# Layer 0's recurrent loop: the order of two transposes, two products on another engine, and the step that makes the gate's products

## The chip, the cores and the metric

The kernel runs on one core of a Trainium2 chip. A core has four compute engines that matter here, each with its own in-order instruction stream: TensorE (PE; its weight loads appear as PEld), VectorE (DVE), ScalarE (ACT) and GpSimd (POOL). SyncE (SP) issues most DMAs. The metric is the device time of one execution in microseconds; lower is better. The kernel before takes 4783.76 us, the median of three runs (4769.75 to 4790.43).

## The reference

Four layers, each with an attention-like part `s` and a feed-forward part whose silu is its gate; the residual `x` becomes `x + s * silu(f)`. Only layer 0 is touched by the change. Its attention part is a state-space recurrence over 512 tokens, with a batch of 8; its feed-forward part is a mixture of eight experts that does not depend on the recurrence at all:

```python
def step(carry, inp):
    state, y_prev = carry
    xBC = silu(xBC_t + y_prev @ W_rxbc.T)
    dtr = silu(dt_t + y_prev @ W_rdt.T)
    ...
    dt = softplus(dtr + dt_bias); dA = exp(dt * A)
    state = state * dA + dt * x_h * B
    y = (state * C).sum(-1) + D_param * x_h
    g = y * silu(z_t)
    yn = g * rsqrt(mean(g * g) + EPS) * norm_w
    return (state, yn), yn @ W_out.T
...
h = relu(einsum('etd,efd->etf', xn, w1) + b1)
y = x + einsum('etf,edf->etd', h, w2) + b2
```

Each step needs the `yn` of the step before it, so the 512 steps are one serial chain.

## The kernel before

`layer0` walks `step(t)` for t = 0 to 511 under a manual schedule: within the loop each engine's instructions stand in the order in which the code writes them. The expert network's work is spread through the loop to fill TensorE's spare time, and whatever of it is left when the last step is issued is made by `ffn.rest` behind the loop. Then the loop's outputs are projected (L546), scaled (L549) and gated into the residual (`gate_residual`, L51 to L53); layer 1 starts from that residual.

**One step.** The last result, `yh` (L414), feeds `norm` and the recurrent product on TensorE (L221). GpSimd makes the root `rh` (L283), VectorE adds up the row `a` (L317), ScalarE applies silu (`ar`, L323), VectorE turns it (`h`, L325). From `h` come `cb` (L339) and `Z`; TensorE sums `cb` into `pag` (L354) and multiplies `Z` with the saved state into `pym` (L361, 64 records). GpSimd meanwhile makes `v`, `e`, `e` and `dec` (L332 to L350), the decay; then `xd` (L351), `zd` (L352) and, late, the new column of `xw` (L402). VectorE ends the step with a run of small operations: `tmp`, its sums `R`, `M`, the turned step size `td`, the turned decay `dA`, the turned state product `ty` (which reads `pym`), then products and sums into the next `yh`, and last the decay of the history `xw` (L423).

The state is not updated in each step. The kernel keeps a history of up to `past` tokens and folds it into the saved state once in eight steps. `past` runs from 5 to 12. A step is **long** where `past` > 8: these are the steps with t % 8 of 1, 2, 3 and 4 from t = 9 on, 252 of them. In long steps the sums `R` are taken in two halves, with `td` between them, and the folding is made: GpSimd's `decayed` (L490) runs at "half 0" ahead of `v`, TensorE's products `us` (L479) at "update".

**The fillers on TensorE.** At "products" each step asks `ffn.products` for up to four matmuls (not where t % 8 is 0) and fills up to seven with `occupy`, matmuls whose result nobody reads. Behind the state product it calls `aside(t)`, in steps that have no `us` products or whose t % 16 is in `ASIDE`, and fills up to four with `occupy`. `aside` makes one of three things: a group of the next projections (`ASIDE` 0 to 3), the two products of the gate z two chunks ahead (`ASIDE` 4; their silu is queued in `gates` for the next two steps), or another call of `ffn.products`.

**The expert network.** 256 jobs (eight experts, 32 token tiles), each of four hidden products with four RELUs on ScalarE (L673, L683), four output products (L656) and one add on VectorE (L691). One call of `products` gives at most four matmuls: either hidden columns or one job's outputs. `activate(RELUS[t % 8])` is at most 18 RELUs in eight steps.

Of the kernel before, what the change touches and what calls it, by code (L numbers as in the profile page):

```python
# [11 lines left out]
ALU = mybir.AluOpType  # L12
# [45 lines left out]
PC = 8  # L58
TC = 16
Q = 8  # L60
ASIDE = {5: 0, 7: 1, 13: 2, 15: 3, 9: 4}
CAP = 40.0
RELUS = [2, 1, 1, 1, 2, 4, 4, 3]
LAG = 5
# [74 lines left out]
def layer0(tc, K, I, dr, xn, s_all, s_out, x, B, T):  # L139
# [10 lines left out]
    nc = tc.nc  # L150
    ident, eps = K["ident"], K["eps"]
    with ExitStack() as ctx:
# [42 lines left out]
        xw = wp.tile([P, 2, B, 32], F32, name="xw")  # L195
        SINCE = (0, 2 * Q + 1)
# [8 lines left out]
        pa, pg, py, pm = pag[:, 0:RW], pag[:, 256:384], pym[:, 0:64], pym[:, 64 : 64 + B]  # L205
# [6 lines left out]
        tt_, stt_ = nc.vector.tensor_tensor, nc.vector.scalar_tensor_tensor  # L212
# [10 lines left out]
        def occupy(n, where):  # L223

            for _ in range(n):
                nc.tensor.matmul(where, ident, K["ones"], start=True, stop=True)  # L226
# [4 lines left out]
        def aside(t):  # L231

            c, r = t // TC + 2, t % TC
            if c * TC < T and r in ASIDE:
                j = ASIDE[r]
                if j == 4:
                    for k in range(2):
                        proj.gate(c, k, ring[k])
                        gates.append(lambda k=k: proj.silu(c, k, ring[k]))
                    return 2  # L240
                proj.group(c, j, ring[j % 2])
                if j == 3:
                    proj.dt(c, pdt)

                def kept():
                    proj.keep(c, j, ring[j % 2])
                    if j == 3:
                        proj.send(c, pdt)

                sums.append((t, kept))  # L250
                return 4
            return ffn.products(t, sums)
# [5 lines left out]
        def turned(src, n, name):  # L258
            t = wk.tile([P, n, 32], F32, name=name)
            nc.vector.transpose(out=t, in_=src)  # L260
            return t

        def small(name, n=2, bufs=2):
            return wk.tile([P, n, B], F32, name=name, bufs=bufs)

        def one_(name):
            return wk.tile([P, 1], F32, name=name)

        def both(v):

            return v.unsqueeze(1).to_broadcast([P, 2, B])
# [15 lines left out]
        def part(t, place):  # L287
            f = parts.pop((t, place), None)
            if f:
                f()  # L290
            return f is not None

        def held(t):

            return max(0, (t - LAG) // Q)
# [6 lines left out]
        def step(t, rt, zt):  # L302
# [23 lines left out]
            now = slice(B * s, B * s + B)  # L326
            C, x = h[:, 0, now], h[:, 2:4, now]
            part(t, "half 0")
            v, dt, dec = one_("v"), one_("dt"), one_("dec")
            e, w, ad = one_("e"), one_("w"), one_("ad")  # L330

# [12 lines left out]
                o += hi - lo  # L344
            nc.vector.tensor_copy(bass.AP(z9.tensor, z9.offset, [list(z9.ap[0]), [9, B]]), C)
            tt_(w, v, Acap, ALU.mult)
            xz, xd, zd = small("xz"), small("xd"), small("zd")
            tt_(xz, x, zt, ALU.mult)
            tt_(ad, w, A, ALU.min)
            nc.gpsimd.tensor_tensor(dec, e, ad, ALU.pow)  # L350
            nc.gpsimd.tensor_tensor(xd, xz, Dp, ALU.mult)  # L351
            nc.gpsimd.tensor_tensor(zd, xw[:, :, :, SINCE[held(t) % 2]], zt, ALU.mult)  # L352
            for j in range(4):
                nc.tensor.matmul(  # L354
                    pg[32 * j : 32 * j + 32, 0 : B * o], K["ones"][:, 0:32], cb[:, 0 : B * o], start=True, stop=True
# [9 lines left out]
            given = 4 if part(t, "update") else 0  # L365
            if not given or t % TC in ASIDE:
                given += aside(t)
# [11 lines left out]
            M = small("M")  # L379

            def total(c):
                nc.vector.tensor_reduce(out=R[:, c], in_=tmp[:, c, :, 0:past], op=ALU.add, axis=AX.X)  # L382

            spread = lambda v, name: turned(v.to_broadcast([P, 32]), 1, name)[:, 0, 0:B]
            long = past > Q
# [5 lines left out]
            td = both(spread(dt, "td"))  # L391
            if long:
                total(1)
            dA = both(spread(dec, "dA"))
            tt_(M, M, td, ALU.mult)
            if long:
                tt_(R, R, zt, ALU.mult)
            occupy(4 - given, pag[:, 384:])
            part(t, "copies")
            ffn.activate(RELUS[t % Q])  # L400
# [1 line left out]
            nc.gpsimd.tensor_tensor(xw[:, :, :, s + 1], td, x, ALU.mult)  # L402
            part(t, "half 1")

            ty = turned(py.rearrange("p (c e) -> p c e", e=32), 2, "ty")
            y = small("y")
            if past:
                tt_(R, R, dA, ALU.mult)
            tt_(zd, zd, dA, ALU.mult)
            tt_(M, M, xd, ALU.add)  # L410
            tt_(y, zd, ty[:, :, 0:B], ALU.mult)
            if past:
                tt_(M, M, R, ALU.add)
# [110 lines left out]
        with tc.manual_schedule():  # L524
            for t in range(T):
                if t % PC == 0:
                    cur = nxt
                    if t + PC < T:
                        nxt = piece(t // PC + 1)
                if t % Q == Q - 1 and t + 1 + LAG < T:  # L530
                    update(t // Q)
                part(t, "start")
                step(t, cur[:, t % PC, :], proj.z[t // TC][:, :, t % TC, :])
            norm(T - 1)
            ffn.rest(sums)
# [1043 lines left out]
```

## Time and profile before

| what | value |
|---|---|
| median of three runs | 4783.76 us |
| the profiled execution | 4780.57 us |
| its span | 4778.8 us |
| PE busy | 4390.6 us (92%) |
| DVE busy | 3478.5 us (73%) |
| ACT busy | 3292.8 us (69%) |
| POOL busy | 2374.4 us (50%) |
| first and last start of `yh` | 123.1 and 2814.4 us |

The profile has one row for each kind of instruction or for each stretch of a timeline: start or count, duration, engine, line of the kernel, operation, output and inputs. A bracket says how long the engine had been idle and what released it. On TensorE one fp32 matmul of the code leaves two records, so the 1024 hidden products appear as 2048. The loop, from the first `yh` to the last, takes 2691.3 us, 5.27 us a step.

### The profile page before, as it was taken

Reading aid. Unit: us, or ns where it says so; the run is one execution under the profiler, and the core shown is the slowest. Engines: PE = TensorE matmul, PEld = TensorE weight load, DVE = VectorE, ACT = ScalarE, POOL = GpSimd, SP = SyncE. Lnnn points to the kernel's source line nnn. Section 1 sums busy time; section 2 is a strip of 40 time slices with the busy share of each in tenths; the row PEclk is TensorE's granted clock in tenths of the full one; section 3 lists DMA queues with packets and bytes.
Section 4 is the critical chain, followed back from the end, with each engine's and each line's share of the span. In section 5 each row is a group of like instructions: output and inputs, shape, how many; then the busy total and the mean of one; then the engine's idle time right before and its main releaser. Section 6 shows DMA issues by size and latency. Waiting matters only on the chain.

```text
span 4778.8 us, 193203 instructions
## 1 busy us (share of the span) xinstructions
PE 4390.6 (92%) x79351; PEld 3273.0 (68%) x79351; DVE 3478.5 (73%) x18350; ACT 3292.8 (69%) x6513; POOL 2374.4 (50%) x5479
## 2 busy tenths in 40 slices
PE   6999999999999999999999987969999888999998
PEld 5777777777777777777777764325556555666666
DVE  4788888888888888888888876457776336777781
ACT  2788888888888888888888854436666124666665
POOL 1555555555555555555555544420001355778782
PEclk6999999999999999999999998869999998999999
DMA  3000000000000000000000032000000520000000
GB/s 93 12 9 16 9 11 14 8 11 13 11 9 16 8 9 16 9 10 15 9 10 9 9 60 66 18 1 2 2 2 2 107 56 1 2 2 2 2 2 18
DMA packets 72713, 81.39 MB, mean 17 GB/s; under 512 B 8844, under 2 KB 55057, under 8 KB 71699
## 3 DMA queue, kind: packets, MB, share of 16 engines
q1 hardware_dynamic: 67116, 65.04, 5.6%
q8 instruction: 622, 10.19, 0.9%
q10 hardware_dynamic: 4710, 3.99, 0.3%
q14 instruction: 265, 2.16, 0.2%
HBM read 52.72 MB, written 16.29 MB: 14 GB/s over the span
## 4 chain that ended last, share of the span: by engine, by line
PE 44%; DVE 34%; POOL 10%; ACT 6%; issue 5%; DMA 1%; SPq 0%; ACTq 0%; POOLq 0%; DVEq 0%
PE pt L959 7%; POOL rh L283 5%; PE ps_s L938 4%; PE pag L354 4%; PE pym L221 4%; DVE a L317 3%; PE po L973 3%; DVE h L325 3%; ACT ar L323 3%; DVE tmp L374 3%; DVE R L382 3%; DVE cb L339 3%; DVE yh L414 2%; PE ph L673 2%; PE py L1126 2%
## 5 line engine op out<-in xcount | busy, mean ns | idle before, releaser
L216 ACT ACT_TABLE_LOAD x1024 | 1313.8, 1283 | 16.5
L283 POOL TENSOR_TENSOR rh<-ms,half 128x1 f32<-128x1 f32 x512 | 280.3, 548 | 708.5 <-DVE ms L280 707.9
L361 PE MATMUL pym<-S,Z 128*8 128x64 f32 x32768 | 551.9, 219 | 0.1
L1257 POOL TENSOR_SCALAR gp<-toe,ng 128x207 f32<-128x207 f32 (+1 forms) x512 | 489.7, 965 | 111.2 <-DVE mn L946 73.3
L959 PE MATMUL pt<-ident,sb 128*128 128x128 f32 x3328 | 498.4, 283 | 13.0 <-ACT pT L962 8.1
L959 PEld LDWEIGHTS pt<-ident,sb 128*128 128x128 f32 x3328 | 356.5, 141 | 208.2 <-ACT pT L964 78.5
L361 PEld LDWEIGHTS pym<-S,Z 128*8 128x8 f32 x32768 | 489.2, 90 | 0.1
L323 ACT ACTIVATE ar<-a 128x129 f32<-128x129 f32 x511 | 159.6, 312 | 437.3 <-DVE a L317 437.1
L962 ACT COPY pT<-pt 128x512 f32<-128x512 f32 (+3 forms) x512 | 255.5, 499 | 243.5 <-PE pt L959 242.2
L226 PE MATMUL pym<-ones,ident 128*128 128x128 f32 x2942 | 417.4, 277 | 0.0
L946 DVE CUSTOM_DVE_ANT_0 sb<-ps_s,gp 128x512 f32<-128x512 f32 x512 | 324.1, 685 | 101.1 <-PE ps_s L938 86.2
L226 PEld LDWEIGHTS pym<-ones,ident 128*128 128x128 f32 x2942 | 369.7, 192 | 0.4 <-DVE ms L280 0.4
L221 PE MATMUL pag<-w_Wr,yh 128*8 128x129 f32 x8176 | 352.0, 277 | 0.0
L952 ACT ACTIVATE sb<-sb,mn 128x512 f32<-128x512 f32 (+3 forms) x512 | 330.6, 646 | 22.9 <-DVE mn L946 17.3
L221 PEld LDWEIGHTS pym<-yh 128*8 128x8 f32 x8192 | 172.6, 154 | 223.8 <-DVE yh L414 215.7
L317 DVE SCALAR_TENSOR_TENSOR a<-pag,rh,rows 128x129 f32<-128x129 f32 x511 | 180.6, 353 | 197.7 <-POOL rh L283 194.6
L683 ACT ACTIVATE hid<-ph,be 128x128 f32<-128x128 f32 x1024 | 311.2, 360 | 12.1 <-PE ph L673 11.9
L221 PE MATMUL pym<-yh 128*8 128x8 f32 x8192 | 231.5, 220 | 85.8 <-DVE yh L414 61.7
L350 POOL TENSOR_TENSOR dec<-e,ad 128x1 f32<-128x1 f32 x512 | 286.5, 560 | 43.6 <-POOL e L334 1.1
L673 PE MATMUL ph<-xhT,ew 128*128 128x128 f32 x2048 | 308.1, 291 | 0.0
L333 POOL TENSOR_TENSOR e<-base,v 128x1 f32<-128x1 f32 x512 | 280.9, 549 | 40.1
L497 ACT ACTIVATE Sd<-S,das 128x64 f32<-128x64 f32 x1008 | 298.2, 397 | 3.0
(365 smaller groups left out, 10551.1 us busy)
## 6 DMA issues: line engine op xcount, KB each, us to landing
cB<-dc SPq DMA_DIRECT2D x16, 1024.0 KB
pd<-stg SPq DMA_DIRECT2D x32, 258.0 KB
rows<-pd SPq DMA_DIRECT2D x256, 32.2 KB
wu<-in_f_up_dram SPq DMA_DIRECT2D x9, 512.0 KB
wd<-in_f_down_dram SPq DMA_DIRECT2D x9, 512.0 KB
rd<-rv SPq DMA_DIRECT2D x1, 3304.0 KB
x<-in_u_dram SPq DMA_DIRECT2D x8, 256.0 KB
w<-in_f_w_dram SPq DMA_DIRECT2D x8, 256.0 KB
```

Of the source, the lines that this page charges most:

```text
L216: nc.scalar.preload_act_table_set(name)
L221: nc.tensor.matmul(out[32 * j : 32 * j + B, :], lhsT, rhs(j), start=(k == 0), stop=(k == 1))
L226: nc.tensor.matmul(where, ident, K["ones"], start=True, stop=True)
L283: nc.gpsimd.tensor_tensor(rh[:, t : t + 1], ms, half, ALU.pow)
L317: stt_(a, pa, rh[:, t - 1 : t], rt, ALU.mult, ALU.add)
L361: nc.tensor.matmul(py[32 * j : 32 * j + B, :], z9[:, B * b : B * b + B], Sq[b % 4][:, b // 4, :, 32 * j : 32 * j + 32], start=(i == 0), st ...
L673: self.nc.tensor.matmul(self.ph[:, f, :], self.w[n][0][:, f * P : (f + 1) * P], self.xhT[:, i * P : (i + 1) * P], start=True, stop=True)
L683: self.nc.scalar.activation(self.hid[n][:, f, :], self.ph[:, f, :], AF.Relu, bias=self.be[:, self.jobs[n][0], f : f + 1])
L946: nc.vector.tensor_tensor_reduce(out=sb[:, 0:L], in0=ps[:, g, 0:L], in1=bias[g], scale=1.0, scalar=3.0e38, op0=ALU.add, op1=ALU.min, accum ...
L952: nc.scalar.activation(sb[:, 0:L], sb[:, 0:L], AF.Exp, scale=-1.0, bias=mn)
L959: nc.tensor.transpose(pt[:, j * P : (j + 1) * P], sb[:, j * P : (j + 1) * P], self.ident)
L1257: nc.gpsimd.tensor_scalar(t[:, k0:k1], toe[:, h, o : o + k1 - k0], gates[b][:, i, h : h + 1], None, ALU.mult)
```

## The change

Five edits in `layer0`:

- The gate's two products move from the steps with t % 16 = 9 to those with t % 16 = 0.
- `zd` on GpSimd is made behind "half 0", ahead of `v`, instead of behind `xd`.
- In steps that are not long, `ty` is turned ahead of `dA`.
- In long steps `M * td` and `M + xd` are made on GpSimd, directly after one another, instead of on VectorE.
- In long steps `ty` keeps its place; in the others both products of M stay on VectorE.

```diff
-ASIDE = {5: 0, 7: 1, 13: 2, 15: 3, 9: 4}
+ASIDE = {0: 4, 5: 0, 7: 1, 13: 2, 15: 3}
...
             part(t, "half 0")
+            zd = small("zd")
+            nc.gpsimd.tensor_tensor(zd, xw[:, :, :, SINCE[held(t) % 2]], zt, ALU.mult)
...
-            xz, xd, zd = small("xz"), small("xd"), small("zd")
+            xz, xd = small("xz"), small("xd")
...
             nc.gpsimd.tensor_tensor(xd, xz, Dp, ALU.mult)
-            nc.gpsimd.tensor_tensor(zd, xw[:, :, :, SINCE[held(t) % 2]], zt, ALU.mult)
...
             if long:
                 total(1)
+            turned_y = lambda: turned(py.rearrange("p (c e) -> p c e", e=32), 2, "ty")
+            if not long:
+                ty = turned_y()
             dA = both(spread(dec, "dA"))
-            tt_(M, M, td, ALU.mult)
             if long:
+                nc.gpsimd.tensor_tensor(M, M, td, ALU.mult)
+                nc.gpsimd.tensor_tensor(M, M, xd, ALU.add)
                 tt_(R, R, zt, ALU.mult)
+            else:
+                tt_(M, M, td, ALU.mult)
...
-            ty = turned(py.rearrange("p (c e) -> p c e", e=32), 2, "ty")
+            if long:
+                ty = turned_y()
...
-            tt_(M, M, xd, ALU.add)
+            if not long:
+                tt_(M, M, xd, ALU.add)
```

## The prediction

> **What bounds the kernel now.** The first view is the slice row of the page: layer 0's loop fills slices 2 to 24 of 40. The timeline's `yh` rows give 2691.3 us from first to last, 5.27 us a step. PE looks 90% busy there, but much of that is `occupy`, which fills waiting time, so busy shares say little. I therefore read the chain of waits over a stretch with a gate step (t % 16 = 9):
>
> ```profile
> 1515.21 0.89 PE pym L361 x64
> 1516.11 1.06 PE us L479 x4
> 1517.16 0.64 PE paside L131 x4
> 1517.80 0.42 PE pym L221 x10
> ```
>
> Columns: start, length, what. Here TensorE decides: the gate's products (L131) stand between the folding products and the next step's L221. Everywhere else the step is a chain through all engines whose end is VectorE's run of small operations. A long step on VectorE, and below it GpSimd beside it (start, length, engine, line, operation, output and inputs):
>
> ```profile
> 1521.48 0.20 DVE L260 STREAM_TRANSPOSE td<-dt 128x32 f32<-128x32 f32 x1
> 1521.61 0.20 DVE L382 TENSOR_REDUCE R<-tmp 128x8 f32<-128x80 f32 x1
> 1521.72 0.20 DVE L260 STREAM_TRANSPOSE dA<-dec 128x32 f32<-128x32 f32 x1
> 1521.85 0.18 DVE L395 TENSOR_TENSOR M<-M,td 128x16 f32<-128x16 f32 x1
> 1521.95 0.16 DVE L397 TENSOR_TENSOR R<-R,z 128x16 f32<-128x16 f32 x1
> 1522.04 0.24 DVE L260 STREAM_TRANSPOSE ty<-pym 128x64 f32<-128x64 f32 x1
> 1522.20 0.13 DVE L408 TENSOR_TENSOR R<-R,dA 128x16 f32<-128x16 f32 x1
> 1522.26 0.16 DVE L409 TENSOR_TENSOR zd<-zd,dA 128x16 f32<-128x16 f32 x1
> 1522.34 0.17 DVE L410 TENSOR_TENSOR M<-M,xd 128x16 f32<-128x16 f32 x1
> 1522.45 0.17 DVE L411 TENSOR_TENSOR y<-zd,ty 128x16 f32<-128x16 f32 x1
> 1522.54 0.17 DVE L413 TENSOR_TENSOR M<-M,R 128x16 f32<-128x16 f32 x1
> 1522.75 0.19 DVE L414 TENSOR_TENSOR yh<-y,M 128x16 f32<-128x16 f32 x1
> ```
>
> ```profile
> 1521.07 0.56 POOL L350 TENSOR_TENSOR dec<-e,ad 128x1 f32<-128x1 f32 x1
> 1521.60 0.22 POOL L351 TENSOR_TENSOR xd<-xz,w_Dp 128x16 f32<-128x16 f32 x1
> 1521.78 0.23 POOL L352 TENSOR_TENSOR zd<-xw,z 128x16 f32<-128x16 f32 x1
> 1521.96 0.24 POOL L402 TENSOR_TENSOR xw<-td,h 128x16 f32<-128x16 f32 x1
> ```
>
> The starts matter, not the lengths. Independent operations start 0.05 to 0.17 us apart; a dependent one starts 0.03 after the other's end: `zd` to `y` is 0.19, `M+R` to `yh` 0.21. What follows the loop is the third view:
>
> ```profile
> 2816.09 10.86 PE L546 MATMUL po<-w_WoT,yh 128*128 128x128 f32 x94
> 2837.16 1.26 POOL L53 TENSOR_TENSOR x<-x,gate 128x512 f32<-128x512 f32 x1
> ```
>
> The last `yh` starts at 2814.36. TensorE projects, and GpSimd's eight gate chunks end at 2838.42, 24.06 us later. No expert work is left by then: the last output product starts at 2805.7.
>
> **Edit 1, the gate's step.** From `yh` to L221 it takes 0.24 us normally and 0.65 after t % 16 = 9 (median of 31), and the rest of the next step (1.32 to `rh`, 0.73 to `ar`) is alike, so all 0.41 comes back. In t % 16 = 9 of the last two chunks an expert call stands in the gate's place, which goes too: 32 x 0.41 = **13 us** gained. In t % 16 = 0 two gate products and two `occupy` replace four matmuls: nothing. The silus of the gate now stand in the ACT streams of t % 16 = 1 and 2, ahead of `ar`; ACT is idle 0.56 to 1.2 us before `ar` in such steps and a silu takes 0.28: nothing.
>
> **But the call is lost to the experts.** At t % 16 = 9 the gate sat in a step that already had `us`; at 0 it takes the place of `ffn.products`. Calls in 16 steps: 14 at "products", four in `aside` (t % 16 = 0, 6, 8, 14), together 18; eight jobs need 16 full ones. After it 17 are left, and some are short because hidden columns may run only four ahead of the RELUs. I stepped the counters (`cols`, `relus`, `outs`) of both through the loop: before, 256 jobs are out at the last step; after, seven instead of eight in 16 steps, and at the end 918 columns and 228 jobs. The changed kernel's instruction order says the same: behind the last step stand 107 hidden and 112 output products, mixed with 57 projections. Inside the loop `occupy` takes their places, so nothing is saved there.
>
> Price: 276 matmuls are 552 records. L546 ran 94 in a row, loads 10.67 us, 0.1135 each: 62.7 us. They start 0.6 after the last `yh` and end at +63.5 (two jobs of lead, so no RELU holds them: four take 1.12 us beside 2.27 us of PE per job with its projections). Then the last add 0.35, its gate silu 0.63, two GpSimd operations of 1.27 and gaps: +67.3, against 24.1. That is **+43 us**. ACT's 12 weight DMA issues (6.6 us in all) formerly lay in gaps; in the new order they stand behind the last gate silu, ahead of a 1.28 us table load and layer 1's root. About 4 us were free there; I take +3 (0 to 4). Tail **+46** (42 to 50).
>
> **Edit 2, long steps.** VectorE loses `M*td` and `M+xd`. `M*td` to `R*z` is 0.05 to 0.075 in the four phases, mean 0.065: gained. `M+xd` fills the time in which `y` waits for `zd`: nothing. The chain on GpSimd: `xd` starts 0.53 after `dec`, +0.18, and a dependent start costs length plus 0.08: `M*td` 0.22, `M+xd` 0.22, wake 0.04, so `M+R` may start 1.27 to 1.36 after `dec` starts. VectorE reaches it at 1.42 (t % 8 = 1) to 1.56: covered, but by 0.06 to 0.2 only; behind it waits `yh`. `xw` (L402) then ends about 1.46 after `dec`, ahead of L423, at 1.70.
>
> Here a rule speaks against the change. The Trainium skill's SBUF — State Buffer (SBUF: two separate sides) says that a GpSimd operation and a VectorE one with two SBUF inputs exclude each other for the whole instruction. By it, two more GpSimd operations of 0.22 would cost up to 0.44 a step, 111 us. The rows above show GpSimd's `zd` over 1521.78 to 1522.01 with `M*td` and `R*z` both starting within it; `M*td` is 0.128 to 0.233 long over all steps, `zd*dA` 0.132 to 0.201. So an overlap costs between 0 and 0.1, not the whole. New overlaps fall on `zd*dA`, `y` and `M+R`; I take 0.025 a step, nearest to the 0.04 by which `zd*dA` exceeds its median. Net 0.04 x 252 = **10 us** gained (16 gained to 34 lost).
>
> **Edit 3, `zd` early.** In long steps it stands between `decayed` and `v`. `decayed` ends 0.22 before `v` in nearly every step, and `zd`'s successor follows 0.21 after its start: it fits, with 0.04 over. In others GpSimd idles 0.8 us there. Nothing; a delay of `v` is covered by 0.1 to 0.27 between `dec` and `dA`.
>
> **Edit 4, `ty` first in short steps.** `pym` ends 0.09 to 0.19 after `td` starts, and VectorE follows TensorE 0.06 after (as `tmp` does). `ty` so starts 0.155 to 0.25 after `td`, `dA` 0.166 later, `R*dA` 0.20 to 0.285 after that. Old sums `td` to `R*dA`: 0.59, 0.535, 0.58, 0.51 (t % 8 = 5, 6, 7, 0); new at the low end 0.615, 0.586, 0.556, 0.52. The wait for `dec` was about as long as that for `pym`. With 0.037 less at `zd*dA` in two phases: 0 to 0.08 lost; I take 0.015 x 256 = **4 us** lost (0 to 20).
>
> **Sum.** -13 - 10 + 4 + 46 = **+27**. On the profiled execution's 4780.57 us, 3.2 below the median shown, that is 4808 us.
>
> **Rivals.** *GpSimd becomes the bound* (0.18). `M+xd` arrives late or the lock bites: if long steps lose 0.1 instead of gaining 0.04, +35: 4843. For it: 0.06 of cover at t % 8 = 1. Against: the lengths above.
> *Not slower: the loop pays for the tail* (0.12). If the end of a long step follows the number of VectorE operations, `M+xd`'s 0.08 counts as well: 0.145 x 252 = 37, with 13 and 5 from the short steps 55, against 43: 4769. It decides from 0.14 us a long step on. Against: `y` starts 0.19 after `zd*dA` whatever stands between.
> *The backlog is hidden* (0.08): if layer 1 could start beside it, 4762. Against: the residual needs every expert.
> *Forecast* (0.62): 4808, its own range 4790 to 4826.
>
> What a measurement of this kernel tells from no change is about 0.5%, 24 us. The forecast lies just beyond: of its 0.62, 0.36 is slower and 0.26 the same. With the rivals: slower 0.54, same 0.39, faster 0.07. Range 4782 to 4842.
>
> **What would show it.** L691 and L656 running some 60 us behind the last `yh`; L221 0.24 after `yh` in every step; the step after the gate 0.4 shorter; long steps 0.04 shorter; `M+R` never waiting for POOL; `dA` in short steps 0.17 behind `ty`. A tail under 30 us, or long steps changed by over 0.1, would prove me wrong.

## The result, and the profile after

The changed kernel takes **4844.21 us**, the median of six runs (4834.32 to 4852.74), beside 4783.97 for the kernel before in the runs beside it: a ratio of **1.013, 95% interval 1.0114 to 1.0145**. It is slower, as forecast, but by 60 us, where 27 were forecast; 4844 lies just outside the range. The profiled execution took 4834.37 us, so the traces differ by 53.8 us (spans 4832.6 and 4778.8), where 27 were forecast, and that is the difference to be explained here.

The top of the page:

```profile
span 4832.6 us, 194069 instructions
PE 4417.9 (91%) x79659; PEld 3298.9 (68%) x79659; DVE 3469.5 (72%) x17846; ACT 3295.2 (68%) x6513; POOL 2488.9 (52%) x5983
```

TensorE's and VectorE's shares went down by a point each while the kernel became slower. Shares can't show what happened; landmarks can. Four of them, from the timelines:

| landmark (us) | before | after | difference |
|---|---|---|---|
| first `yh` to last `yh` | 2691.2 | 2682.9 | -8.3 |
| last `yh` | 2814.36 | 2804.36 | -10.0 |
| last `yh` to the end of the last gate chunk (residual) | 24.1 | 77.2 | **+53.1** |
| residual to layer 1's first projection (`ps_p`) | 5.4 | 18.4 | **+13.0** |
| the rest | | | -2.3 |

The loop became shorter, but by less than half of what was forecast (19). The tail became longer, and by more (46 forecast for both tail rows).

**The gate's step.** TensorE's timeline of the step t % 16 = 9 (its rows are start, length, engine, line, operation, output and inputs; the bracket is idle time and its releaser):

```profile
1510.63 1.08 PE L362 MATMUL pym<-S,Z 128*8 128x64 f32 x64
1511.64 1.13 PE L488 MATMUL us<-xs,bs 32*128 32x256 f32 x4
1512.93 0.44 PE L221 MATMUL pym<-yh 128*8 128x8 f32 x16 [0.17 <-DVE yh L423]
```

No L131 row is left between the folding products and L221. Before, L221 had to wait behind the gate's products though `yh` was ready; now TensorE waits 0.17 us for `yh` (start 1512.69). The steps with t % 16 = 10 went from 5.73 to 5.19 us in the mean.

**A long step**, the same one (t % 16 = 9), on VectorE and below it on GpSimd:

```profile
1511.68 0.20 DVE L260 STREAM_TRANSPOSE dA<-dec 128x32 f32<-128x32 f32 x1
1511.81 0.23 DVE L402 TENSOR_TENSOR R<-R,z 128x16 f32<-128x16 f32 x1
1511.95 0.23 DVE L260 STREAM_TRANSPOSE ty<-pym 128x64 f32<-128x64 f32 x1
1512.12 0.13 DVE L416 TENSOR_TENSOR R<-R,dA 128x16 f32<-128x16 f32 x1
1512.17 0.19 DVE L417 TENSOR_TENSOR zd<-zd,dA 128x16 f32<-128x16 f32 x1
1512.40 0.17 DVE L420 TENSOR_TENSOR y<-zd,ty 128x16 f32<-128x16 f32 x1
1512.49 0.17 DVE L422 TENSOR_TENSOR M<-M,R 128x16 f32<-128x16 f32 x1
```

```profile
1511.78 0.22 POOL L400 TENSOR_TENSOR M<-M,td 128x16 f32<-128x16 f32 x1
1512.08 0.25 POOL L401 TENSOR_TENSOR M<-M,xd 128x16 f32<-128x16 f32 x1
1512.30 0.22 POOL L409 TENSOR_TENSOR xw<-td,h 128x16 f32<-128x16 f32 x1
```

GpSimd's `M+xd` ends at 1512.33, 0.16 before VectorE starts `M+R`: GpSimd is not late. But `zd*dA` now runs beside GpSimd, lasts 0.19, and `y` starts 0.23 after it, where 0.19 was shown before.

**A short step** (t % 8 = 6), first of the kernel before, then of the changed one:

```profile
1542.46 0.20 DVE L260 STREAM_TRANSPOSE td<-dt 128x32 f32<-128x32 f32 x1
1542.64 0.21 DVE L260 STREAM_TRANSPOSE dA<-dec 128x32 f32<-128x32 f32 x1
1542.78 0.13 DVE L395 TENSOR_TENSOR M<-M,td 128x16 f32<-128x16 f32 x1
1542.83 0.24 DVE L260 STREAM_TRANSPOSE ty<-pym 128x64 f32<-128x64 f32 x1
1542.99 0.13 DVE L408 TENSOR_TENSOR R<-R,dA 128x16 f32<-128x16 f32 x1
1543.05 0.20 DVE L409 TENSOR_TENSOR zd<-zd,dA 128x16 f32<-128x16 f32 x1
```

```profile
1537.56 0.20 DVE L260 STREAM_TRANSPOSE td<-dt 128x32 f32<-128x32 f32 x1
1537.79 0.25 DVE L260 STREAM_TRANSPOSE ty<-pym 128x64 f32<-128x64 f32 x1
1537.96 0.17 DVE L260 STREAM_TRANSPOSE dA<-dec 128x32 f32<-128x32 f32 x1
1538.05 0.13 DVE L404 TENSOR_TENSOR M<-M,td 128x16 f32<-128x16 f32 x1
1538.16 0.18 DVE L416 TENSOR_TENSOR R<-R,dA 128x16 f32<-128x16 f32 x1
1538.26 0.17 DVE L417 TENSOR_TENSOR zd<-zd,dA 128x16 f32<-128x16 f32 x1
```

From `td` to `zd*dA` it was 0.59 us and is now 0.70. Before, `dA` started 0.18 behind `td`, and `R*dA` followed `ty` by 0.16, when `dA` was long done. Now `ty` starts 0.23 behind `td`, because it waits for `pym` (TensorE's last product into it ends at 1537.72), and `dA` comes last: `R*dA` waits 0.20 for it with nothing but `M*td` to do meanwhile. After that wait `R*dA` takes 0.18 instead of 0.13, and its successor starts 0.10 behind it instead of 0.06.

**The tail.** TensorE behind the loop:

```profile
2869.12 1.16 PE L682 MATMUL ph<-xhT,ew 128*128 128x128 f32 x8
2870.11 1.06 PE L665 MATMUL po<-ew,hid 128*128 128x128 f32 x8
2871.00 0.61 PE L555 MATMUL po<-w_WoT,yh 128*128 128x128 f32 x4
2871.57 1.16 PE L682 MATMUL ph<-xhT,ew 128*128 128x128 f32 x8
2873.15 1.16 PE L665 MATMUL po<-ew,hid 128*128 128x128 f32 x8 [0.42 <-DVE xn L700]
2874.92 1.16 PE L665 MATMUL po<-ew,hid 128*128 128x128 f32 x8 [0.61 <-DVE xn L700]
2876.61 1.13 PE L665 MATMUL po<-ew,hid 128*128 128x128 f32 x8 [0.54 <-DVE xn L700]
```

```profile
2872.55 0.29 DVE L22 BATCH_NORM_STATS2 ln_st<-x 128x6 f32<-128x128 f32 x1 [3.44 <-POOL x L53]
2872.76 0.34 DVE L700 SCALAR_TENSOR_TENSOR xn<-po,coef,xn 128x128 f32<-128x128 f32 x1
```

Two expert jobs (hidden, output, projection) start 2.45 us apart. The last three output products wait in turn for VectorE's add `xn` (L700), and the first of these adds stands behind a norm's statistics that waited 3.44 for GpSimd's `x`. The residual ends at 2881.53 (the last L53 on GpSimd, 2880.27 + 1.26). Then come the lines of ScalarE and of SyncE, and TensorE again:

```profile
2878.55 0.94 ACTq L1415 DMA_DIRECT2D w_cn_w<-in_cn_w_dram  x2
...
2885.66 0.44 ACTq L1415 DMA_DIRECT2D w_f_wg<-in_f_wg_dram  x1
2887.35 0.33 ACTq L1415 DMA_DIRECT2D w_f_wd<-in_f_wd_dram  x1
2887.71 1.28 ACT L25 ACT_TABLE_LOAD   x1 [8.86 <-DMA w_a_q<-in_a_q_dram]
2889.01 0.32 ACT L25 ACTIVATE ln_rs<-ln_mv,eps 128x32 f32<-128x32 f32 x1
```

```profile
2891.13 0.31 SPq L1157 DMA_DIRECT2D oneh<-in_k_buckets_dram  x1
```

```profile
2891.20 0.45 PE L43 MATMUL pt<-ident,xn 128*128 128x128 f32 x1 [13.46 <-DVE xn L34]
2896.84 1.55 PE L1160 MATMUL ps_r<-oneh,w_a_rel 40*16 40x414 f32 x2 [5.19 <-DMA oneh<-in_k_buckets_dram]
2898.32 0.90 PE L43 MATMUL pt<-ident,xn 128*128 128x128 f32 x3
2899.90 3.78 PE L730 MATMUL ps_p<-xT,w_a_w 128*128 128x512 f32 x4 [0.68 <-ACT xT L44]
```

Layer 1's root `ln_rs` starts 7.48 us after the residual, where it was 1.35 before: ScalarE's twelve weight loads were issued from 2878.55 to 2887.68, 9.1 us with the pauses between them. And behind the first of layer 1's transposes (`pt`) stands `ps_r`, a product for layer 3's table of positions, made by `position_rows`; the other three transposes wait for it. Its input `oneh` is issued by SyncE behind the weight loads, at 2891.13. Before, `oneh` was issued at 2810.52 and the product was made in a gap, when no one waited, and ScalarE had issued its loads ahead of the silus of the gate and between them (product and root before):

```profile
2829.46 0.86 PE L1151 MATMUL ps_r<-oneh,w_a_rel 40*16 40x414 f32 x2
2839.77 0.32 ACT L25 ACTIVATE ln_rs<-ln_mv,eps 128x32 f32<-128x32 f32 x1 [4.52 <-DVE ln_mv L23]
```

The late root and the late product together are 6.1 (ScalarE) + 5.2 (the wait) + 1.5 (the product) = 12.8 of the 13.0 us.

### The profile page after: what moved, and what is told of

It reads as the page before. It is cut to its first block, busy times and chain, and to the rows that moved or that the text cites. A ratio compares the mean times of both kernels' runs of the same rounds, so it can differ in the third digit from the quotient of the medians.

```text
span 4832.6 us, 194069 instructions
## 1 busy us (share of the span) xinstructions
PE 4417.9 (91%) x79659; PEld 3298.9 (68%) x79659; DVE 3469.5 (72%) x17846; ACT 3295.2 (68%) x6513; POOL 2488.9 (52%) x5983
## 4 chain that ended last, share of the span: by engine, by line
PE 46%; DVE 35%; POOL 8%; ACT 6%; issue 5%; DMA 1%; SPq 0%; ACTq 0%; POOLq 0%; DVEq 0%
PE pt L968 7%; PE ps_s L947 4%; POOL rh L283 4%; PE pag L355 4%; PE pym L221 3%; PE po L982 3%; DVE tmp L375 3%; DVE a L317 3%; DVE R L383 3%; DVE h L325 3%; ACT ar L323 3%; DVE cb L341 2%; PE ph L682 2%; PE pym L226 2%; DVE ty L260 2%
## 5 line engine op out<-in xcount | busy, mean ns | idle before, releaser
L226 PE MATMUL pym<-ones,ident 128*128 128x128 f32 x3308 | 458.0, 277 | 0.0
L226 PEld LDWEIGHTS pym<-ones,ident 128*128 128x128 f32 x3308 | 410.4, 192 | 0.0
L221 PE MATMUL pag<-w_Wr,yh 128*8 128x129 f32 x8176 | 351.2, 277 | 0.0
L221 PEld LDWEIGHTS pym<-yh 128*8 128x8 f32 x8192 | 173.1, 154 | 245.3 <-DVE yh L423 244.6
L221 PE MATMUL pym<-yh 128*8 128x8 f32 x8192 | 231.5, 219 | 98.2 <-DVE yh L423 91.8
L665 PE MATMUL po<-ew,hid 128*128 128x128 f32 x2048 | 294.6, 287 | 4.1 <-DVE xn L700 4.1
```

What stands on the lines that cost most here:

```text
L221: nc.tensor.matmul(out[32 * j : 32 * j + B, :], lhsT, rhs(j), start=(k == 0), stop=(k == 1))
```

## The experiments

Theory 1: the change is slower because the expert call lost at t % 16 = 0 leaves 28 jobs behind the loop. Rivals: the loop's own edits cost it (the short steps, or GpSimd in the long ones), or the queues behind the loop do. In all of them steps are compared by this table, made from the starts of `yh` in each profile (mean us from `yh` to `yh`, t from 9 on; "gate" is t % 16 = 10, the step behind the old gate step, "long" the other long steps):

| kernel | edits in the loop | short (251) | long (220) | gate (32) | loop |
|---|---|---|---|---|---|
| before | none | 5.141 | 5.342 | 5.729 | 2691.2 |
| e8 | `zd` early | 5.115 | 5.348 | 5.727 | 2685.8 |
| e3 | `ty` first | 5.204 | 5.340 | 5.727 | 2706.8 |
| e2 | gate's step | 5.140 | 5.341 | 5.251 | 2675.2 |
| e4 | `zd` early, Pool products | 5.107 | 5.310 | 5.663 | 2673.4 |
| e1 | as after, old gate step | 5.205 | 5.309 | 5.665 | 2697.9 |
| after | all | 5.205 | 5.310 | 5.186 | 2682.9 |
| e5 | as after, gate at "products" | 5.210 | 5.309 | 5.193 | 2684.8 |
| e6 | e5 without `ty` first | 5.110 | 5.312 | 5.196 | 2659.7 |
| e7 | e6 with `M+xd` on VectorE | 5.112 | 5.274 | 5.165 | 2651.0 |

The changed kernel and e9 to e12 have the same loop; their five loops lie between 2682.9 and 2683.9 us, which is how far a difference in this table can be trusted.

**e1: the changed kernel with the old gate step.**

```diff
-ASIDE = {0: 4, 5: 0, 7: 1, 13: 2, 15: 3}
+ASIDE = {5: 0, 7: 1, 13: 2, 15: 3, 9: 4}
```

> The changed kernel with the gate's products back at t % 16 = 9, all else as changed. Theory 1 (the lost expert call leaves 28 jobs behind the loop, and these make the loss): from the last yh to the residual 24 us again instead of 77, layer 1 starts 5.4 us after it instead of 18.4; the loop gets the gate's 13 us back. About +7 us against before (short steps +16, long -9), ratio 1.0015. Rival 2 (the loss lies in the new order within the steps, VectorE waiting): still +40 us or more, ratio 1.009.

Measured: 4793.98 us, ratio 1.0042 (1.0026 to 1.0058). Last `yh` to residual is 23.8 us again, residual to `ps_p` 5.4. So both tail rows hang on that one table entry. What is left is mostly the loop, 6.7 us longer than before; the two spans differ by 9.9 (4788.7 and 4778.8), while the medians differ by 16.8, with an interval from 12 to 28.

**e2: the gate's step alone**, the same line the other way round, in the kernel before.

> The kernel before with the gate's products at t % 16 = 0 and nothing else. Theory 1: loop -13 us, tail +53 and start of layer 1 +13: +53 us against before, ratio 1.011. Rival 2: the gate's step alone is a gain, -13 us, ratio 0.997.

Measured: 4833.07, ratio 1.0119 (1.0099 to 1.0138). The loop is 16.0 us shorter, nearly all of it in the steps behind the old gate step (32 x 0.478 = 15.3), and the residual ends 76.8 us after the last `yh`. This one line holds nearly all of the change's loss, though it is the edit that helps the loop most.

**e3: `ty` first in short steps, alone; e4: `zd` early and the Pool products, alone; e8: `zd` early, alone.** Each is the part of the shown diff that it names, in the kernel before.

> The kernel before with ty turned ahead of dA in steps that are not long, nothing else. Theory 1: dA then stands directly ahead of R*dA, which needs it and starts 0.20 us after it, so each of these 256 steps is 0.06 longer: +16 us, ratio 1.003. What I predicted blind was +4 us, ratio 1.001. Rival 2: over +30 us.

> The kernel before with zd made early and with M*td and M+xd of long steps on GpSimd, nothing else. Theory 1: td to R*dA 0.07 shorter, zd*dA to y 0.03 longer beside GpSimd's M+xd, net 0.037 x 252 = -9 us, ratio 0.998. Rival 2 (M+R waits for GpSimd): +10 us or more, ratio 1.002.

> The kernel before with zd made ahead of v on GpSimd, nothing else. Theory 1: v starts when it did; in two of the four short phases zd*dA to y shortens by up to 0.037 us (128 steps): 0 to -5 us, ratio 0.999 to 1.000. Rival (zd delays v behind decayed in long steps): +10 us, ratio 1.002.

Measured: e3 4794.69, ratio 1.0039 (1.0019 to 1.0059), short steps 0.063 longer; e4 4764.15, 0.9983 (0.9964 to 1.0002; the time alone is not clear of no change, the loop is 17.8 shorter), long steps 0.032 shorter and short ones 0.034; e8 4771.2, 0.9987 (0.9978 to 0.9996), short steps 0.026 shorter. The edits don't add up in the short steps: `zd` early is worth 0.026 there, but with `ty` first it is worth nothing (5.204 in e3, 5.205 in e1). The kernel before shows why. At t % 8 = 5 and 6, `zd*dA` runs beside GpSimd's `xw` and lasts 0.197; at t % 8 = 7, `M*td` runs beside `zd` and lasts 0.228. With `zd` early these are 0.17 and 0.15. With `ty` first (e3), `zd*dA` comes later than `xw` and lasts 0.169 at t % 8 = 5 and 6 already. `M*td` still takes 0.211 at t % 8 = 7, but most of that lies inside the time in which `R*dA` waits for `dA`: taking `zd` out of its way brings `R*dA` forward by 0.026, where it was 0.086 in the old order. From `td` to `yh` that leaves 0.012 at t % 8 = 7, and the other three phases are 0.003 to 0.008 longer.

**e5: the gate's products in the old step, but at "products"**, ahead of the state product, in place of two `occupy`. It keeps the expert call at t % 16 = 0, and L221 need not wait for the gate. It tests whether the loop's gain can be had without the tail.

```diff
-ASIDE = {0: 4, 5: 0, 7: 1, 13: 2, 15: 3}
+ASIDE = {5: 0, 7: 1, 13: 2, 15: 3}
...
-                    occupy(7 - ffn.products(t, sums), idle)
+                    made = ffn.products(t, sums)
+                    c = t // TC + 2
+                    if t % TC == 9 and c * TC < T:
+                        for k in range(2):
+                            proj.gate(c, k, ring[k])
+                        made += 2
+                    occupy(7 - made, idle)
...
+            if t % TC == 9 and (t // TC + 2) * TC < T:
+                for k in range(2):
+                    gates.append(lambda k=k, c=t // TC + 2: proj.silu(c, k, ring[k]))
```

> The changed kernel, but the gate's two products stand at 'products' in steps with t % 16 = 9, in place of two occupy matmuls, and their silus follow in the next two steps as before; so t % 16 = 0 has its expert call again and no gate stands behind the us products. Theory 1: no job is left behind the loop and L221 starts 0.24 us after yh everywhere: gate -13, long -9, short +16: -6 us against before, ratio 0.999. Rival (the gate's products at t % 16 = 9 cost their 0.41 us wherever they stand in that step): +7 us, ratio 1.0015.

Measured: 4768.78, ratio 0.9983 (0.9974 to 0.9992). The loop is about as long as in the changed kernel (2684.8 beside 2682.9), the residual ends 23.8 us after the last `yh` and `ps_p` follows 5.4 us later. The gain at the gate and the tail are separate things; made in place of `occupy`, the gate's products cost next to nothing.

**e6: e5 with `ty` at its old place in all steps; e7: e6 with `M+xd` on VectorE again**, so that GpSimd has only `M*td`.

```diff
-            if not long:
-                ty = turned_y()
...
-            if long:
-                ty = turned_y()
+            ty = turned_y()
```

```diff
                 nc.gpsimd.tensor_tensor(M, M, td, ALU.mult)
-                nc.gpsimd.tensor_tensor(M, M, xd, ALU.add)
...
-            if not long:
-                tt_(M, M, xd, ALU.add)
+            tt_(M, M, xd, ALU.add)
```

> The same, with ty behind dA in all steps as before (so: gate at 'products', zd early, both products of M on GpSimd in long steps). Theory 1: -13 - 9 = -22 us against before, ratio 0.9953. Rival: the gains overlap, or the gate's place costs again: -9 us, ratio 0.998.

> As e6, but only M*td of long steps on GpSimd and M+xd back on VectorE, where it fits into the 0.19 us in which y waits for zd*dA. Theory 1 (GpSimd's M+xd beside zd*dA and y costs 0.03 to 0.06 us a step): 0.03 x 252 = 7 us faster than e6, -29 us against before, ratio 0.994. Rival (VectorE's count of operations decides): slower than e6 by 0.08 x 252 = 20 us, ratio 0.9995.

Measured: e6 4751.3, ratio 0.9937 (0.9924 to 0.9951); e7 **4737.44, ratio 0.9914 (0.9901 to 0.9928)**, which is faster than both kernels. `ty` first cost 25 us of loop here (2684.8 to 2659.7), where it cost 15.6 alone, for the reason above. `M+xd` on GpSimd cost 9: a long step of e7 on VectorE:

```profile
1505.01 0.13 DVE L421 TENSOR_TENSOR R<-R,dA 128x16 f32<-128x16 f32 x1
1505.06 0.16 DVE L422 TENSOR_TENSOR zd<-zd,dA 128x16 f32<-128x16 f32 x1
1505.14 0.17 DVE L423 TENSOR_TENSOR M<-M,xd 128x16 f32<-128x16 f32 x1
1505.26 0.18 DVE L424 TENSOR_TENSOR y<-zd,ty 128x16 f32<-128x16 f32 x1
```

`M+xd` lies in the time in which `y` waits for `zd*dA` (0.20 here), so VectorE makes it for nothing; on GpSimd it lies beside `zd*dA` and lengthens that wait to 0.23.

**e9: `position_rows` behind layer 1's attention; e10: all weight loads on SyncE; e11: both; e12: the changed kernel again beside them.** These test the 13 us between the residual and `ps_p`.

```diff
-            rd = position_rows(tc, W, dr)
...
+                rd = position_rows(tc, W, dr)
```

```diff
-        (nc.sync if n % 2 == 0 else nc.scalar).dma_start(out=t, in_=I[name])
+        nc.sync.dma_start(out=t, in_=I[name])
```

> The changed kernel with layer 3's position rows (the loads of oneh, the ps_r matmuls, their copies) made behind layer 1's attention instead of ahead of it, nothing else. Theory 1 (5 to 7 of the 13 us by which layer 1 starts later after the residual are TensorE's in-order wait for the oneh load at ps_r): 5 to 7 us less than the changed kernel, ratio to before 1.011. Rival (the wait only uncovers another, such as the load of layer 1's weights): no change, 1.0125.

> The changed kernel with all weight loads behind layer 0 issued by SyncE, none by ScalarE. Theory 1 (6 of the 13 us are ScalarE's issues ahead of the table load and the root of layer 1's norm): ln_rs follows the residual by about 1.4 us instead of 7.5; but SyncE issues 12 more at 0.4 us ahead of oneh, 5 us, so of the gain little is left unless the wait at ps_r is gone too: 0 to 3 us less than the changed kernel. Rival: 6 us less.

> e9 and e10 together. Theory 1: layer 1 starts about 5.4 us after the residual as before instead of 18.4: 11 to 13 us less than the changed kernel, ratio to before about 1.010. Rival (the weights themselves land late): 6 us less or fewer.

> The changed kernel itself, for comparison on the same chip: ratio to before 1.0125.

Measured: e9 4880.07, ratio 1.0206 (1.0189 to 1.0224); e10 4850.66, 1.0144 (1.0127 to 1.0161); e11 4878.32, 1.0199 (1.0184 to 1.0214); e12 4839.38, 1.012 (1.0103 to 1.0137). In total time none gained: e9 and e11 came out 47 and 51 us above what was expected of them, and e10 11 us above e12, where 0 to 3 below it were expected. In the stretch that they were made for they do tell: residual to `ps_p` is 17.5 us in e12, 14.4 in e9, 19.5 in e10 and 5.35 in e11, as before the change. With one cause taken away the other still holds TensorE: in e9 the root is as late as before (7.5), and ScalarE's further loads hold its copy `xT` too; in e10 the root is early (1.3 us after the residual) but `oneh` comes later still. In e11 neither is left. TensorE of e10, then of e11:

```profile
2901.23 1.56 PE L1160 MATMUL ps_r<-oneh,w_a_rel 40*16 40x414 f32 x2 [12.21 <-DMA oneh<-in_k_buckets_dram]
```

```profile
2886.62 3.78 PE L730 MATMUL ps_p<-xT,w_a_w 128*128 128x512 f32 x4 [0.72 <-ACT xT L44]
```

The waits of e9 between 2890 and 3260 (engine, what waits, for what: total, times, longest, in us) show what was paid for it:

```profile
ACT o L44 <- DMA rd<-rv: 38.7, 1, 38.7
...
DVE hb L807 <- DMA rd<-rv: 35.2, 1, 35.2
```

`position_rows` also writes its table to memory (`rd<-rv`, 3304 KB). Moved, that transfer is issued at 3046.5, in layer 1, and two engines wait for it; in the changed kernel it is issued at 2899.42 and no such wait stands in the list. So the 13 us are explained, but these two moves are no way to get them back; the gate's step is (e5).

## Why the prediction was right or wrong

The mechanism was right, and its sizes were not: of the 27 us that the traces show beyond the forecast, 20 are the two tail terms and 11 the loop, less 4 outside both. One rival's number, 4843, nearly meets the measured 4844; that is chance, for its cause (GpSimd as the bound) did not come true.

- **Direction and main cause: right.** The lost expert call and 28 jobs behind the loop outweigh what the loop gains (e1, e2, e5).
- **Edit 1, 13 us gained: right, somewhat low.** e2 gives 16.0; t % 16 = 10 came back by 0.48, not 0.41.
- **The tail to the residual, +43: right in kind, mis-sized; +53 measured.** The step that failed is "four take 1.12 us beside 2.27 us of PE per job", with "+67.3" as its end; the residual came at 77.2. Jobs stand 2.45 us apart where records of 0.1135, taken from 94 projections in a row, gave 2.27: 5.0 us over 28 jobs; why a record takes longer in the mixed order was not tried. Every fourth job TensorE waits 0.4 for VectorE's add, queued behind a norm's statistics that wait 3.4 for GpSimd's `x`; four jobs so take 10.28 instead of 9.80, 3.4 over seven such waits. And the last two output products wait 0.61 + 0.54 for the add of the one before. Together these are 9.6 of the 9.9 us missed. The sum took TensorE as the only limit behind the loop.
- **The root behind the weight loads, "+3 (0 to 4)": mis-sized, and half of it not seen; +13 measured.** The 4 us that were to be free there were free: the last gate silu ends at 2878.85, and 1.35 after the residual would be 2882.88. What failed is "6.6 us in all": the twelve issues themselves take 5.1, but with the pauses between them they last 9.1 us, and the root is 6.1 later. And the DMAs that SyncE issues behind the loop were not followed: `oneh` stands behind the weight loads, and the product that reads it stands ahead of three of layer 1's transposes on TensorE's in-order queue. e11 shows that the two together are all of it.
- **Edit 2, 10 us gained: right in the sum.** e4 gives 220 x 0.032 and, from the gate's steps, 32 x 0.066: 9.1. Its overlap term was taken as 0.025; `zd*dA` to `y` grew by 0.03. But the edit was priced as one, and its halves have opposite signs: `M*td` on GpSimd gains, `M+xd` there loses 9 (e6, e7).
- **Edit 3, nothing: right for the changed kernel, not by itself.** Alone it gains 5.4 (e8), as it takes GpSimd's work out of the way of `M*td` and `zd*dA`; with `ty` first `zd*dA` is clear of it in any case and `M*td` lies in a wait, and in sum nothing is left to gain.
- **Edit 4, 4 us lost (0 to 20): right sign, mis-sized; 16 measured.** 0.0645 a step, not 0.015. From `td` to `R*dA` it takes 0.033 more, twice the 0.016 of the low end that was taken. From `R*dA` to `zd*dA` it takes 0.039 more (0.054 to 0.093), which the working left as it was: here that distance is short only where `R*dA` did not itself have to wait. From `zd*dA` to `yh` 0.007 come back, where 0.018 were taken.
- **Rival "GpSimd becomes the bound": wrong**; `M+xd` ends 0.16 to 0.22 before `M+R`, and long steps are shorter. **Rival "the loop pays": wrong**; a long step gains 0.032, far from 0.14. **Rival "the backlog is hidden": wrong**; the residual waits for all of it.

The sum after the fact, in the loop: -16 - 9 + 16 = -9, against -8.3 in the profile; behind it +53.1 and +13.0. The rest, -1.7 between the start and the loop and -2.3 behind `ps_p`, is no more than the scatter of that code from trace to trace: among the kernels that have it unchanged the first `yh` starts between 120.2 and 124.6, and from `ps_p` to the end it takes 1923 to 1940 us.

## What to carry to other kernels

Before moving work out of a slot, ask what the slot it goes to was doing: here a filler slot held a useful call, and a slot of pure filler (e5) stood in the same step. What is left behind a loop is paid there in full, with the adds and waits of its whole chain (2.57 us a job here, not TensorE's 2.27 alone), and it pushes every DMA and every odd product that was queued into a gap to a place where something waits for them; so follow each in-order queue past the end of the loop. In a run of small operations, put an independent one between an operation and the one that waits for it: here `M+xd` on VectorE was free inside such a wait (e7), and beside it on GpSimd it cost 0.03 us a step (e6).

## What the runs showed of the hardware

- **GpSimd and VectorE beside each other cost little here, but not nothing.** In the kernel before, `zd*dA` with 0.175 us of overlap with GpSimd's `xw` lasts 0.197 (mean of t % 8 = 5 and 6) and 0.159 to 0.161 without any (t % 8 = 2 and 3); `M*td` lies beside GpSimd for all of its length at t % 8 = 5, 6 and 7 and lasts 0.133, 0.133 and 0.228. In the changed kernel `R*dA` lasts 0.126 beside `M+xd` at t % 8 = 1 and 2, no longer than alone, but at t % 8 = 4 it lasts 0.199 in the 46 steps in which `M+xd` ends and `xw` begins beside it, and 0.132 in the other 16. The rule weighed in the prediction (the Trainium skill, SBUF — State Buffer, SBUF: two separate sides), that such operations exclude each other for the whole instruction, would by estimate hold `zd*dA` up by some 0.17; it is 0.04 longer, and the other cases lie between 0 and 0.1. Which part of an operation collides was not tried.
- **`R*dA` is slower to let the next operation go when it comes off a wait.** At 128x16 and with no GpSimd operation beside it, it is 0.13 long and its successor 0.054 behind it where `dA` was long done (before, t % 8 = 2 to 4); 0.18 and 0.093 where it had just waited for `dA` (changed kernel, t % 8 = 5 to 7). Over 256 steps the 0.04 is 10 us. No run isolates the cause.
